# Four-direction selective scan with a mixture of experts and attention behind it: the row directions first and last, the normalisation of a batch's tokens in two halves

## The chip, the cores and the metric

The kernel runs on one core of a Trainium2 chip, in one launch. The metric is the device time of that core in microseconds; a kernel is run several times and the median counts. All data are float32.

## The reference, cut to what matters

The input is 4 images of 384 channels and 32 x 32 places; the 1024 places are the tokens. Two layers follow each other.

```python
xs = stack([x0, x1, x0[::-1], x1[::-1]])      # 4 directions: rows, columns, both reversed
dt, Bs, Cs = projections of xs per direction   # dt through softplus
h = h * exp(dt * A) + (dt * u) * B             # per token, 16 states for each channel
y = sum_n h * C
y = y0 + y2[::-1] + transpose(y1 + y3[::-1])   # the four directions added at their places
x = x + gelu(layernorm(y) * w + b)             # layer 0, first part
x = x + sum over 2 of 4 experts: gate * (gelu(ln(x) W1 + b1) W2 + b2)
x = x + attention(ln(x))                       # layer 1: 8 heads, q = k = v
x = x + kron-factored feed-forward(ln(x))
```

The sum of the directions is taken before the layer normalisation, which needs all 384 channels of a token but no other token.

## The kernel before, in words

**The scan (scan_layer, L196).** Channels lie on partitions in blocks of 32, with 4 of the 16 states beside each other. The work is a list of 32 units (L252): batch b, direction k from 0 to 3, and half i of the 1024 tokens, in which k = 0 and 1 run forward and k = 2 and 3 backward. Directions 0 and 2 go by rows and directions 1 and 3 by columns, so that a unit of 0 or 2 adds to one half of the tokens, and one of 1 or 3 to half of the columns of every row. A unit has three chunks of 128 channels (chunk, L401). In a chunk POOL multiplies dt*u by B (L432), ACT takes the exponential (L441), DVE runs the recurrence (L446), POOL or DVE multiplies by C (L460, L453), and PE adds up the states (L467) into acc; DVE adds acc into y (L294 for the first direction, L298 for the others). While a unit runs, the projection of the next one (project, L305) is made piecewise between the chunks; its results go to DRAM and come back spread over partitions (dtr, L416, and bcs, L342), on SP's queue. The PSUM of the scan is two banks "da" and a ring of two banks "ps", which acc, the projections and the normalisations take in turn.

**Between batches.** Ahead of a batch's last unit start (L223) loads and normalises the next input, in two passes of 512 tokens (layernorm, L157: mean by matmuls L164, subtraction L166, squares L173, variance L179, inverse root L150 and L151, spreading L187, multiplication L192). Behind a batch's last unit finish (L236) normalises y in two such passes, takes the GELU of 1024 tokens for each of three channel groups (L239), loads the input again (L246), adds on POOL (L247) and stores x1 to DRAM (L248). The GELU needs another table of ACT than the exponential; exp_again (L143) loads the first one again.

**The tail.** For each batch, tail_batch (L489) runs the experts, the combination, the attention and the last layers beside the scan of the next batch; for the last batch all this comes behind the scan. route (L611) calls spread (L616): it reads x1 back two token blocks at a time (L629), transposes each block on PE and takes the gate's scores (L635, L637), copies both out of the bank "p" (ACT L641, DVE L642), takes mean and variance (L643, L644), and after all eight blocks the inverse root; less_mean (L540) gives minus mean times rstd; places (L676) works out with many small DVE instructions where each token goes; and 16 indirect DMAs on POOL (L664) put the rows there. experts (L817) works through 11 slots (matmuls L889 and L905). combine (L916) fetches the results by indirect DMAs (L935) and adds them; prologue (L953) normalises, with less_mean again. attention (L974) has four steps of two heads; behind each, divide (L1026) adds the two partial sums of the softmax (L1028), inverts them and multiplies (L1045). last_layers (L1077) ends the batch.

**What sets the order.** Each engine takes its instructions in the order of its queue. The queues are made when the program is built, by a scheduler with a simulated timeline that takes ready instructions by priority; route, combine with prologue, and last_layers have a priority that is raised by 20000, and place_behind holds parts of project behind a given instruction. SBUF and PSUM tiles come from rings with a fixed number of buffers (bx 6, dtr 7, k2 6; the tail's banks s, o and p are 1 each), and the next user of a ring waits for the last one. The tail takes its tiles in the order of the program, so the routing of batch b + 1 takes its buffers behind the attention of batch b.

Of the kernel before, what the change touches and what calls it, by code (L numbers as in the profile page):

```python
# [9 lines left out]
F32 = mybir.dt.float32  # L10
I32 = mybir.dt.int32
AF = mybir.ActivationFunctionType
ALU = mybir.AluOpType
AX = mybir.AxisListType
# [3 lines left out]
P = 128  # L18
B = 4
D = 384  # L20
# [3 lines left out]
HF = 512  # L24
NH = L // HF

KG = 4
NS = 16
R = 12
XD = R + 2 * NS  # L30

NE = 4
# [16 lines left out]
MB = L // P  # L49
# [61 lines left out]
def halves(i):  # L111
    return slice(i * HF, (i + 1) * HF)


class Body:
# [80 lines left out]
    def scan_layer(self, x1, between):  # L196

        nc, tc, a = self.nc, self.tc, self.a
        with ExitStack() as ctx:
            wp = ctx.enter_context(tc.tile_pool(name="s_w", bufs=1))  # L200
            work = ctx.enter_context(tc.tile_pool(name="s_work", bufs=1))
# [31 lines left out]
                self.layernorm(x, x, self.eps6, psum, work, parts=[0])  # L233
                return x

            def finish(b, y):  # L236
                self.layernorm(y, y, self.eps5, psum, work)
                for c in range(DC):
                    ins = nc.scalar.activation(  # L239
                        y[:, c, :], y[:, c, :], AF.Gelu,  # L240
                        bias=self.col("lnb", c), scale=self.col("lnw", c),
                    ).ins
                    rows = slice(c * P, (c + 1) * P)
                    for i in range(NH):
                        x = work.tile([P, HF], F32, tag="k2", name="x", bufs=6)
                        nc.sync.dma_start(out=x, in_=a["x"][b][rows, halves(i)])  # L246
                        nc.gpsimd.tensor_add(x, x, y[:, c, halves(i)])  # L247
                        nc.sync.dma_start(out=x1[b][rows, halves(i)], in_=x)  # L248
                self.exp_again(ins)


            units = [  # L252
                (b, k, i)
                for b in range(B)
                for k in range(KG)
                for i in (range(NH) if k < 2 else reversed(range(NH)))
            ]
            us = {0: start(0)}
# [7 lines left out]
            for n, unit in enumerate(units):  # L266
                b, k, i = unit
                fed, ahead = ahead, []
                project = iter(())
                if n + 1 < len(units):  # L270
                    nb = units[n + 1][0]
                    if nb not in us:
                        us[nb] = start(nb)
                    project = self.project(units[n + 1], us[nb], wx, work, dram, psum, ahead)
                    next(project)
                if n % NH == 0:
                    carry = wp.tile([P, NB * NG], F32, tag=f"carry{n // NH % 2}", name="carry")
                if k == 0 and i == 0:
                    y = work.tile([P, DC, L], F32, tag="y", name="y")
                for c in range(DC):  # L280
                    acc = psum.tile([P, HF], F32, tag="ps", name="acc")
                    for _ in self.chunk(
                        unit, n % NH == 0, c, fed, carry, nega, sel, acc, work, dap
                    ):
                        next(project, None)
                    if k % 2 == 0:
                        ys = y[:, c, halves(i)]
                        out = acc
                    else:
                        w = slice(i * (HW // NH), (i + 1) * (HW // NH))  # L290
                        ys = y[:, c, :].rearrange("p (h w) -> p h w", h=HW)[:, :, w]
                        out = acc.rearrange("p (w h) -> p h w", h=HW)
                    if k == 0:
                        nc.vector.scalar_tensor_tensor(  # L294
                            ys, us[b][:, c, halves(i)], dsum[:, c : c + 1], out, op0=ALU.mult, op1=ALU.add
                        )
                    else:
                        nc.vector.tensor_add(ys, ys, out)  # L298
                if k == KG - 1 and b not in self.under_way:
                    self.under_way[b] = fed[2]  # L300
                if n + 1 == len(units) or units[n + 1][0] != b:
                    finish(b, y)
                    between(b)

    def project(self, unit, u, wx, work, dram, psum, made):  # L305

# [233 lines left out]
    def less_mean(self, mean, rstd, room, tag):  # L540

        less = room.tile([P, MB], tag, "less")
        self.nc.vector.scalar_tensor_tensor(less, mean, -1.0, rstd, op0=ALU.mult, op1=ALU.mult)
        return less


# [69 lines left out]
    def spread(self, b, x1, room):  # L616


        nc = self.nc
# [4 lines left out]
        sc = room.tile([P, MB, NE], "sc", "sc")  # L624


        for m in range(0, MB, 2):
            x = room.tile([P, DC, 2 * P], "k4", "x")
            nc.sync.dma_start(out=x, in_=src[:, :, m * P : (m + 2) * P])  # L629
            xt = room.tile([P, 2, D], "k4", "xt")  # L630
            for o in range(2):
                ps = room.bank("p", "tt_ps")
                cols = slice(o * P, (o + 1) * P)
                for c in range(DC):
                    nc.tensor.transpose(ps[:, c * P : (c + 1) * P], x[:, c, cols], self.ident)  # L635
                for c in range(DC):
                    nc.tensor.matmul(  # L637
                        ps[:, D : D + NE], x[:, c, cols], self.wg[:, c, :],
                        start=(c == 0), stop=(c == DC - 1),
                    )  # L640
                nc.scalar.copy(xt[:, o, :], ps[:, :D])  # L641
                nc.vector.tensor_copy(sc[:, m + o, :], ps[:, D : D + NE])  # L642
                nc.vector.bn_stats(st[:, m + o, :], xt[:, o, :])  # L643
                nc.vector.bn_aggr(mv[:, m + o, :], st[:, m + o, :])  # L644
            nc.sync.dma_start(out=self.tokens(b)[:, m : m + 2, :], in_=xt)
# [328 lines left out]
    def attention(self, xc, sums, room):  # L974
# [50 lines left out]

        def divide(t, att):  # L1026
            inv = room.tile([P, 2 * MB], "inv", "inv")
            nc.vector.tensor_add(inv, sums[:, t, :, 0], sums[:, t, :, 1])  # L1028
            nc.vector.reciprocal(inv, inv)
            ps = room.bank("p", "inv_ps")  # L1030
            nc.tensor.matmul(ps[: 2 * MB, :P], inv, self.ident, start=True, stop=True)
            rows = room.tile([2 * MB, P], "inv_rows", "inv_rows")
            nc.vector.tensor_copy(rows, ps[: 2 * MB, :P])
            for i in range(NH):
                ps = room.bank("p", "bc_ps")
                for j in range(HF // P):
                    m = i * (HF // P) + j
                    for o in range(2):
                        at = 2 * m + o
                        nc.tensor.matmul(  # L1040
                            ps[o * HD : (o + 1) * HD, j * P : (j + 1) * P],
                            self.ident[: 2 * MB, at : at + 1].to_broadcast([2 * MB, HD]),
                            rows, start=True, stop=True,
                        )
                nc.vector.tensor_mul(att[:, halves(i)], att[:, halves(i)], ps)  # L1045
# [370 lines left out]
```

## Time and profile before

| | us |
|---|---|
| median of 3 runs | 4451.01 |
| lowest and highest | 4446.85, 4462.27 |
| the profiled execution's own time | 4452.07 |
| its span, first to last instruction | 4450.2 |

| engine | busy us | share of the span |
|---|---|---|
| PE (matmul) | 3462.1 | 78% |
| POOL | 3050.0 | 69% |
| DVE | 2980.1 | 67% |
| ACT | 2469.7 | 55% |

| place in the span | us |
|---|---|
| last add into y, batch 0, 1, 2, 3 | 759, 1678, 2644, 3569 |
| first expert matmul, batch 0, 1, 2, 3 | 935, 1995, 3046, 3696 |
| first score of the attention (L1015), batch 0, 1, 2, 3 | 1462, 2520, 3567, 4195 |

Read the second table with the third: the shares are means over a first part in which the scan runs (to 3570 us) and a last one in which it has ended. A typical unit beside no tail takes 83 to 91 us (batch 0), beside the experts 97 to 108, and the longest are those at a change of batch (161 and 163 us for the first units of batches 1 and 2).

### The profile page before, as it was taken

What the parts mean: (1) busy time and instruction counts of PE and PEld (TensorE: products, weight loads), DVE (VectorE), ACT (ScalarE), POOL (GpSimd) and SP (SyncE); (2) the same over time, 40 slices, a digit from 0 to 9 for tenths busy, and PEclk for the clock granted to TensorE, in tenths of its full rate; (3) what the DMA queues carried; (4) which work ended last, traced back from release to release, by engine and by line L of the source; (5) the groups of instructions that cost most, each with busy time, mean ns of one, the idle gap of its engine ahead of it and who ended that gap; (6) DMA issues with size and microseconds to landing.
All of it is one profiled execution on the core that took longest, in us unless ns stands there. A gap on an engine that the chain in (4) does not pass through costs nothing. (4 is left out here: it accounts for less than half of the span.)

```text
span 4450.2 us, 47090 instructions
## 1 busy us (share of the span) xinstructions
PE 3462.1 (78%) x13980; PEld 1644.5 (37%) x13980; DVE 2980.1 (67%) x4252; ACT 2469.7 (55%) x4380; POOL 3050.0 (69%) x1475
## 2 busy tenths in 40 slices
PE   6545554579995887669998688758998699999897
PEld 2111111245552222325555222214555334566333
DVE  5889998778887876978787777988787720020002
ACT  4545554456664766466666477466666453325354
POOL 4999999689988877779888689879888710000100
PEclk7766665579997998679999899869999899999898
DMA  4444453468785533357779434446778534344300
GB/s 121 119 124 114 129 162 91 134 225 233 217 253 169 164 93 116 117 174 217 209 229 274 134 99 120 123 145 193 215 212 261 171 106 139 123 135 164 102 17 15
DMA packets 404760, 684.81 MB, mean 154 GB/s; under 512 B 50960, under 2 KB 206480, under 8 KB 404496
## 3 DMA queue, kind: packets, MB, share of 16 engines
q1 hardware_dynamic: 395184, 655.37, 50.0%
q0 software_dynamic: 8192, 25.17, 1.7%
q8 instruction: 112, 1.84, 0.2%
q14 instruction: 152, 1.25, 0.1%
q10 hardware_dynamic: 1120, 1.18, 0.1%
HBM read 561.47 MB, written 120.06 MB: 153 GB/s over the span
## 5 line engine op out<-in xcount | busy, mean ns | idle before, releaser
L432 POOL TENSOR_TENSOR bx<-dtr,bcs 128x1024 f32<-128x1024 f32 x768 | 1793.5, 2362 | 211.5 <-PE acc L467 118.2
L441 ACT ACTIVATE da<-dtr,nega 128x512 f32<-128x512 f32 x1536 | 1045.8, 691 | 1013.9 <-DVE bx L453 637.7
L460 POOL TENSOR_TENSOR bx<-bx,bcs 128x1024 f32<-128x1024 f32 x384 | 904.0, 2360 | 216.9 <-DVE bx L446 94.9
L467 PE MATMUL acc<-bx,sel 128*32 128x512 f32 x3072 | 518.6, 712 | 304.2 <-POOL bx L460 258.4
L889 PE MATMUL h_ps<-xc,w 128*128 128x256 f32 (+1 forms) x3168 | 665.2, 364 | 43.6 <-DVE xc L871 21.1
L905 PE MATMUL y_ps<-w,hs 128*128 128x384 f32 x1824 | 644.1, 505 | 44.3 <-ACT hs L898 40.3
L889 PEld LDWEIGHTS h_ps<-xc,w 128*128 128x128 f32 x3168 | 547.4, 196 | 228.6 <-issue 92.0
L446 DVE TENSOR_TENSOR_SCAN bx<-da,carry,bx 128x512 f32<-128x512 f32 x384 | 473.9, 1269 | 125.1 <-ACT da L441 61.9
L446 DVE TENSOR_TENSOR_SCAN da<-da,carry,bx 128x512 f32<-128x512 f32 x384 | 477.3, 1273 | 70.6 <-ACT da L441 61.3
L446 DVE TENSOR_TENSOR_SCAN bx<-da,bx 128x512 f32<-128x512 f32 x384 | 451.8, 1209 | 102.6 <-POOL bx L432 61.3
L453 DVE TENSOR_TENSOR bx<-da,bcs 128x512 f32<-128x512 f32 x768 | 511.3, 680 | 4.5
L446 DVE TENSOR_TENSOR_SCAN da<-da,bx 128x512 f32<-128x512 f32 x384 | 455.7, 1219 | 74.5 <-ACT da L441 62.9
L905 PEld LDWEIGHTS y_ps<-w,hs 128*128 128x128 f32 x1824 | 348.6, 196 | 339.6 <-issue 78.2
L1020 ACT ACTIVATE ex<-s_ps 128x512 f32<-128x512 f32 x512 | 299.2, 590 | 207.1 <-PE s_ps L1015 206.1
L1015 PE MATMUL s_ps<-w 64*128 64x512 f32 x1024 | 307.6, 675 | 83.0 <-ACT ex L1020 83.0
L467 PEld LDWEIGHTS acc<-bx,sel 128*32 128x32 f32 x3072 | 78.6, 116 | 606.1 <-POOL bx L460 371.0
L1064 PE MATMUL o_acc<-ex,vt 128*64 128x512 f32 x1024 | 295.3, 657 | 0.6 <-ACT att L1072 0.5
L894 ACT ACTIVATE hs<-h_ps,bb 128x256 f32<-128x256 f32 (+1 forms) x528 | 193.6, 449 | 148.5 <-PE h_ps L889 148.3
L1105 POOL TENSOR_TENSOR xt<-xt,wb 128x3072 f32<-128x3072 f32 x4 | 26.7, 6686 | 310.4 <-DMA wb<-in_wb 310.4
L909 DVE TENSOR_TENSOR y<-y_ps,bb 128x384 f32<-128x384 f32 x76 | 41.6, 548 | 244.0 <-PE y_ps L905 244.0
L926 POOL TENSOR_TENSOR diag<-ident,g_picked 128x1024 f32<-128x1024 f32 x8 | 15.0, 1895 | 243.1 <-PE xc_ps L868 223.8
L1015 PEld LDWEIGHTS s_ps<-w 64*128 64x128 f32 x1024 | 80.9, 192 | 257.6 <-ACT ex L1020 153.4
(215 smaller groups left out, 4026.3 us busy)
## 6 DMA issues: line engine op xcount, KB each, us to landing
w<-in_w SPq DMA_DIRECT2D x352, 576.0 KB
dtr<-dd SPq DMA_DIRECT2D x1536, 128.0 KB
bcs<-rows SPq DMA_DIRECT2D x512, 128.0 KB
dd<-one_e SPq DMA_DIRECT2D x96, 256.0 KB
dd<-mag SPq DMA_DIRECT2D x96, 256.0 KB
rows<-zero SPq DMA_DIRECT2D x76, 192.0 KB
xs<-rows SPq DMA_DIRECT2D x32, 384.0 KB
made<-y SPq DMA_DIRECT2D x32, 384.0 KB
```

Source lines behind the costliest of these rows:

```text
L432: pool = nc.gpsimd.tensor_mul(bx, dtr[q][1], bc[:, 0].unsqueeze(1).to_broadcast([P, 2, HF])).ins
L441: nc.scalar.activation(da, dtr[q][0][:, j, :], AF.Exp, scale=nega[:, col : col + 1])
L446: nc.vector.tensor_tensor_scan(run(h), run(da), run(bx[:, j, :]), 0.0 if first else hold, ALU.mult, ALU.add,)
L453: dve = nc.vector.tensor_mul(bx[:, j, :], h, cg).ins
L460: pool = nc.gpsimd.tensor_mul(bx, bx, cg.unsqueeze(1).to_broadcast([P, 2, HF])).ins
L467: nc.tensor.matmul(acc[lo : lo + DB, :], sel, out[q][:, j, :], start=(g == 0), stop=(g == NG - 1),)
L889: nc.tensor.matmul(ps[:, r, :], w1[(f + r) // wf][:, c, (f + r) % wf * P : ((f + r) % wf + 1) * P], xc[:, c, :], start=(c == 0), stop=(c = ...
L894: nc.scalar.activation(hs[:, f + r, :], ps[:, r, :], AF.Identity, bias=bb[:, f + r : f + r + 1])
L905: nc.tensor.matmul(out[:, :D], hs[:, f, t * P : (t + 1) * P], w2[f // wf][:, f % wf, :], start=(f == 0), stop=(f == FC - 1),)
L1015: nc.tensor.matmul(ps[:, o, :], w[rows, j * P : (j + 1) * P], w[rows, halves(i)], start=True, stop=True,)
L1020: ins = nc.scalar.activation(ex[:, o, :], ps[:, o, :], AF.Exp, scale=HD**-0.5, accum_out=sums[:, t, 2 * j + o, i : i + 1],).ins
L1064: ins = nc.tensor.matmul(out[cols, :], made[t][1][:, j, cols], ex[:, o, :], start=(j == 0), stop=(j == MB - 1),).ins
```

## The change

Four things are changed.

1. The directions are taken in the order 0, 1, 3, 2 (ORDER), so that the last one goes by rows, backwards: its first unit completes tokens 512 to 1023, its second one tokens 0 to 511.
2. finish takes a half i and is called after each of the two units of the last direction: one normalising pass, three GELUs on 512 columns, three loads, adds and stores, and a table load back. Its first call stands ahead of the batch's last unit.
3. spread reads the token blocks 4 to 7 before 0 to 3. In batch 0 a pair of blocks goes into the double bank "s" and is copied out by one ACT and one DVE instruction.
4. less_mean copies rstd to PSUM by ACT before its DVE instruction, and divide adds the two sums by a reduction instead of an addition of two operands.

The working out of the places is as it was.

```diff
 KG = 4
+ORDER = (0, 1, 3, 2)
...
-            def finish(b, y):
-                self.layernorm(y, y, self.eps5, psum, work)
+            def finish(b, y, i):
+                self.layernorm(y, y, self.eps5, psum, work, parts=[i])
                 for c in range(DC):
                     ins = nc.scalar.activation(
-                        y[:, c, :], y[:, c, :], AF.Gelu,
+                        y[:, c, halves(i)], y[:, c, halves(i)], AF.Gelu,
                         bias=self.col("lnb", c), scale=self.col("lnw", c),
                     ).ins
                     rows = slice(c * P, (c + 1) * P)
-                    for i in range(NH):
-                        x = work.tile([P, HF], F32, tag="k2", name="x", bufs=6)
-                        nc.sync.dma_start(out=x, in_=a["x"][b][rows, halves(i)])
-                        nc.gpsimd.tensor_add(x, x, y[:, c, halves(i)])
-                        nc.sync.dma_start(out=x1[b][rows, halves(i)], in_=x)
+                    x = work.tile([P, HF], F32, tag="k2", name="x", bufs=6)
+                    nc.sync.dma_start(out=x, in_=a["x"][b][rows, halves(i)])
+                    nc.gpsimd.tensor_add(x, x, y[:, c, halves(i)])
+                    nc.sync.dma_start(out=x1[b][rows, halves(i)], in_=x)
                 self.exp_again(ins)
...
-                for k in range(KG)
+                for k in ORDER
...
-                if k == KG - 1 and b not in self.under_way:
-                    self.under_way[b] = fed[2]
-                if n + 1 == len(units) or units[n + 1][0] != b:
-                    finish(b, y)
-                    between(b)
+                if k == ORDER[-1]:
+                    self.under_way.setdefault(b, fed[2])
+                    finish(b, y, i)
+                    if n + 1 == len(units) or units[n + 1][0] != b:
+                        between(b)
...
         less = room.tile([P, MB], tag, "less")
-        self.nc.vector.scalar_tensor_tensor(less, mean, -1.0, rstd, op0=ALU.mult, op1=ALU.mult)
+        ps = room.bank("p", "less_ps")[:, :MB]
+        self.nc.scalar.copy(ps, rstd)
+        self.nc.vector.scalar_tensor_tensor(less, mean, -1.0, ps, op0=ALU.mult, op1=ALU.mult)
...
-        for m in range(0, MB, 2):
+        for m in [*range(MB // 2, MB, 2), *range(0, MB // 2, 2)]:
...
+            both = room.two("tt_ps") if b == 0 else None
             for o in range(2):
-                ps = room.bank("p", "tt_ps")
+                ps = room.bank("p", "tt_ps") if both is None else both[:, o, :]
...
-                nc.scalar.copy(xt[:, o, :], ps[:, :D])
-                nc.vector.tensor_copy(sc[:, m + o, :], ps[:, D : D + NE])
+                if both is None:
+                    nc.scalar.copy(xt[:, o, :], ps[:, :D])
+                    nc.vector.tensor_copy(sc[:, m + o, :], ps[:, D : D + NE])
+            if both is not None:
+                nc.scalar.copy(xt, both[:, :, :D])
+                nc.vector.tensor_copy(sc[:, m : m + 2, :], both[:, :, D : D + NE])
+            for o in range(2):
...
-            nc.vector.tensor_add(inv, sums[:, t, :, 0], sums[:, t, :, 1])
+            nc.vector.tensor_reduce(inv, sums[:, t], AX.X, ALU.add)
```

## The prediction

> **What bounds the kernel now.** I read the page's forty slices first, then busy time by stretch, the list of waits, and the timelines of the places that the diff touches.
>
> ```profile
> PE   6545554579995887669998688758998699999897
> DVE  5889998778887876978787777988787720020002
> POOL 4999999689988877779888689879888710000100
> PEclk7766665579997998679999899869999899999898
> ```
>
> A slice is 111 us. Up to slice 32 (3570 us) POOL and DVE are busy: the scan. From there PE is at 9. So two chains run side by side: the scan (32 units, paced by POOL and DVE) and the tail (experts, attention, last layers of the batch before). The program ends when PE has done what tail work is left when the scan ends.
>
> ```profile
> 3575.00:3600.00 25.00, 25.00 (x115) 13.85 (x114) 3.77 (x6) 10.14 (x26) 0.00 (x0) 0.94 0.22 72
> ...
> 3675.00:3700.00 25.00, 17.30 (x64) 7.08 (x63) 1.39 (x3) 7.03 (x24) 5.48 (x6) 0.86 0.61 236
> 3700.00:3725.00 25.00, 25.00 (x121) 14.48 (x119) 1.66 (x3) 8.83 (x24) 0.00 (x0) 1.00 0.26 72
> ```
>
> Columns: stretch, its length, then busy us of PE, weight loads, DVE, ACT, POOL. Behind the scan PE is full but for some 17 us between 3600 and 3700, in which the last batch is normalised and routed. So what counts is (a) when the scan ends, (b) how far the tail has come by then, (c) those 17 us.
>
> The last output add of batch 0 is at 759.1 us; then, by the timeline:
>
> ```profile
> 759.88 4.76 PE L164 MATMUL ln_mean<-y,ones 128*128 128x512 f32 x6 [0.89 <-DVE y L298]
> ...
> 778.75 1.87 DVE L192 TENSOR_TENSOR y<-y,ln_rows 128x512 f32<-128x512 f32 x3
> ...
> 793.97 7.41 POOL L247 TENSOR_TENSOR x<-x,y 128x512 f32<-128x512 f32 x6 [16.22 <-ACT y L239]
> ...
> 809.46 0.90 PE L635 MATMUL tt_ps<-ident,x 128*128 128x128 f32 x3 [9.12 <-DMA x<-x]
> ```
> ```profile
> 935.14 5.49 PE L889 MATMUL h_ps<-xc,w 128*128 128x256 f32 x12 [1.05 <-DVE xc L871]
> ```
>
> Two normalising passes, one per half of the tokens, come one behind the other (760 to 781, then to 794), then the GELU, the adds, the write of x1, its re-reading, eight transposing rounds to 842, the places, the indirect writes, and 176 us after the last add the first expert matmul. The tail is a serial chain from there: experts 935 to 1383, attention to 1775, routing of the next batch, experts 1995, 3046. So a lead won at 935 is carried to 3570.
>
> ```profile
> 1426.00 12.68 DVE L543 SCALAR_TENSOR_TENSOR less<-mv,rstd 128x8 f32<-128x8 f32 x1 [0.61 <-ACT rstd L151]
> ```
> ```profile
> 1425.90 4.63 POOL L432 TENSOR_TENSOR bx<-dtr,bcs 128x1024 f32<-128x1024 f32 x2
> 1430.51 1.25 POOL L388 TENSOR_TENSOR lnw<-lnw,mag 128x512 f32<-128x512 f32 x1
> 1431.73 6.92 POOL L432 TENSOR_TENSOR bx<-dtr,bcs 128x1024 f32<-128x1024 f32 x3
> 1441.19 2.35 POOL L460 TENSOR_TENSOR bx<-bx,bcs 128x1024 f32<-128x1024 f32 x1 [2.54 <-DVE bx L446]
> ```
>
> An instruction on 8 numbers a partition holds DVE for 12.68 us: exactly until POOL, after three multiplies without a gap, pauses at 1438.6. Then POOL in its turn waits for the scans.
>
> ```profile
> 2817.36 10.53 DVE L1028 TENSOR_TENSOR inv<-sums 128x16 f32<-128x16 f32 x1 [0.98 <-ACT ex L1020]
> ```
> ```profile
> 1599.89 7.01 POOL L432 TENSOR_TENSOR bx<-dtr,bcs 128x1024 f32<-128x1024 f32 x3 [24.05 <-PE acc L467]
> ```
>
> The first is the same in the attention's division. The second is the scan's own loss: ahead of a batch's last unit the next input gets two normalising passes, and the accumulator of that unit comes behind them in a ring of two PSUM banks.
>
> **What the Trainium skill says.** SBUF — State Buffer, section "Who interferes with whom": a DVE instruction with two SBUF inputs is blocked whole by a GpSimd instruction that reads SBUF; one with at most one SBUF input isn't, and tensor_reduce never is. The trace agrees: L543 (two SBUF inputs) 12.68 us against 0.15 at its best, while L453 (one input in PSUM) has a mean of 680 ns beside a busy POOL. ScalarE: Activation LUTs, section "What ACT_TABLE_LOAD costs": a load of about 1283 ns, 2.66 us for a switch with its drain; here the load is 1283 ns, a drain is not shown.
>
> **The change, part by part.** *Smaller stalls in DVE.* In less_mean one input moves to PSUM, in divide two become one reduce. L543 took 12.68, 11.62 and 10.80 us in the scan's time, 0.15 otherwise: 34.6 us gone, less three ACT copies of 128x8 (0.2 us each, from L151) and a hand-over (below 0.4 us): 33 us of the tail's chain. The copy waits for the single bank "p", which nothing else holds there. L1028: 10.53 once, 1.84, 1.42, 2.35 and 0.49 in other divisions; only each attention's last is on the tail's chain: 10 us. For the scan these stalls are worth POOL's idle time behind them: 12.5 us after 1438, 5.4 at 2510, 8.5 at 2836, 12.2 after 3547, together 38.6; some would have come otherwise, I take **30**.
>
> *Finish by halves.* Per half: 3 mean matmuls, 3 subtracts, 3 squares, 12 small matmuls, 2 ACT steps, 4 spreading matmuls, 3 multiplies, 3 GELUs, 3 loads and 3 stores on SP, 3 adds on POOL. Nothing but the tables is added: 4 more switches each way, 8 x 1.28 = 10 us of ACT (21 with the skill's drain, 0 where GELU neighbours GELU), hidden: ACT is 55% busy; uncovered I charge 2. Three GELUs on 512 columns instead of 1024 cost half plus overhead, +2 us in all. Behind batch 0's last add only one pass is left: the adds end at about 786 and not 801 (15 us); of the eight rounds (33 us) four are done during the last unit: 17 us. So the experts begin **32 us** earlier. A pair of rounds for one (only batch 0) saves a handover or two, counted at nothing. The re-reading of the first half needs only its own stores; if it waited for all, the 17 are lost.
>
> *Where the moved half goes.* It stands ahead of the last unit, in front of the two passes of the next input: three passes there, one after. A pass is some 14 to 16 us; 6 bx buffers cover the accumulator for about 14 (six multiplies of 2.36). Loss in sum: before 24.1 and 20.5 (input) plus 16.2, 22.5, 19.5 (finish, POOL's wait for the GELU); after, about 16 more at the first place and 16 less at the second: **0**, from -16 to +16 for each of three batches. In the last batch one pass comes into the scan unaccompanied, covered by the buffers: +4 (0 to 16). On SP the three stores wait for POOL with the dtr loads of the next chunk queued behind; cover is one chunk, about 30 us; if it is gone, 5 to 7 us each (waits seen at L432 for dtr: 5.6, 6.7).
>
> *Order of directions.* The same eight units with the same instructions: 0. The sums of units 4 to 7 swap strided for plain views (L298: 659 to 692 ns for both).
>
> **Sum**, against the profiled 4452.1 us (span 4450.2, 1.9 around it; median of the runs 4451.0). Scan's end: -30 +4 +5 (more tail beside it) = -21, at 3549. Tail: -32 -33 -10 = -75, attention of batch 2 at 3492 instead of 3567. It then has 57 us beside the scan and not 3; in 296 us of the attention before it PE did about 175 us of its matmuls (a quarter of 307.6+295.3+96.6), 0.6 per us: 54 x 0.6 = 32 us of PE work done ahead. Idle behind the scan: of 17 us I take back 6. -21 -32 -6 = -59: 4393, as median **4392**.
>
> **Rivals.** *A, the boundary stalls fall too:* the three waits of POOL for GELU (58 us) go, and the three passes overlap. For: pass 2 began at 777.8 under pass 1. Against: the ring. Another -45: 4347. *B, the lead isn't cashed:* the re-reading waits for both halves and the experts' stage, with PE at 9, eats the rest; only DVE's release counts: -25: 4426. *C, nothing to measure:* B, and the queues made anew lose 20 us: 4447. *D, slower:* the ring decides. Three passes hold the accumulator 16 us longer in three batches (+48) and 16 in the last, POOL's in-order wait for the GELU stays where it was, so nothing is given back: scan -30 +48 +16 +5 = +39. The scan's delay then reaches the routing of batch 1, which has only some 60 us between x1 (1727) and its first transpose (1792): the tail is gated and loses its lead but for some 25 us x 0.6 = 15. +24: 4475. It decides when POOL's waits ahead of the last units pass about 40 us in each batch with the later ones at 20 as before.
>
> **Chances.** Forecast 0.45 (own range 4358 to 4415), A 0.15, B 0.15, C 0.10, D 0.15. About 0.3% (13 us) is what a measurement can tell here. Faster 0.75, same 0.10, slower 0.15. The range goes from A's middle, 4340, to just short of D, 4460.
>
> **What would show it.** L543 and L1028 at 0.2 us everywhere; first L889 near 903; adds of batch 0's second half done by 790; attention of batch 2 near 3490; last scan near 3550. Wrong if POOL's wait ahead of the last unit grows past 40 us while the one behind it stays, or if the first half's transposes come no earlier than the second's.

## The result and the profile after

| | before | after |
|---|---|---|
| median, us | 4451.24 (13 runs) | 4440.3 (13 runs) |
| lowest and highest | 4446.85, 4466.64 | 4429.68, 4447.66 |
| the profiled execution, its span | 4452.07, 4450.2 | 4435.07, 4433.2 |
| ratio to before, 95% interval | | 0.9966 [0.9957, 0.9975] |

The change gains 11 us in the medians and 17 between the two profiled executions. The forecast was 59: right in sign, wrong in size. The forty slices of the kernel after, in the same order of rows as before:

```profile
PE   6545555479886887579987888569998789999797
DVE  5889997878777868968786857977878740020002
POOL 4999996889878968788888859678988931000100
PEclk7766665589997998689998888769999899999898
```

The picture is the same: a scan up to slice 32, then a full PE. Taking the same marks in both traces (last add into y, first expert matmul, first score matmul) shows where the parts of the sum went:

| us in the span | before | forecast | after |
|---|---|---|---|
| last add of batch 0 | 760 | 760 | 793 |
| first expert matmul, batch 0 | 935 | 903 | 922 |
| first score, batch 0 / 1 / 2 | 1462 / 2520 / 3567 | – / – / 3492 | 1441 / 2468 / 3522 |
| last add of batch 3 (the scan's end) | 3570 | 3549 | 3582 |
| last matmul of the last experts | 4146 | 4087 | 4129 |

Busy time by stretch, from the scan's end to the last expert matmul (columns: stretch, its length, then busy us of PE, weight loads, DVE, ACT, POOL, the granted clock, DMA share, GB/s), first of before:

```profile
3570.00:4146.00 576.00, 555.57 (x2425) 320.88 (x2421) 72.23 (x192) 252.97 (x507) 33.33 (x25) 0.98 0.41 136
```

and of after:

```profile
3582.00:4129.00 547.00, 520.90 (x2257) 308.14 (x2255) 68.16 (x187) 230.43 (x444) 29.65 (x22) 0.97 0.42 139
```

168 matmuls fewer are left when the scan ends, and the stretch is 29 us shorter. But it begins 12 us later: -29 + 12 = -17.

**The stalls of DVE are gone.** The instructions of the two lines that took 12.68 and 10.53 us (count, then min, median and max in ns):

```profile
L547 DVE SCALAR_TENSOR_TENSOR less<-mv,less_ps x8: 147/158/164, 841.5 to 4160.0; 128x8 f32<-128x8 f32 x8
```
```profile
L1039 DVE TENSOR_REDUCE inv<-sums x16: 161/186/188, 1505.8 to 4336.5; 128x16 f32<-128x32 f32 x16
```

None is above 0.19 us, as the Trainium skill has it (SBUF — State Buffer, "Who interferes with whom": one SBUF input, or a reduction, doesn't contend).

**The changes of batch cost more.** POOL's timeline of after, at the three places ahead of a batch's last unit:

```profile
683.26 3.73 POOL L248 TENSOR_TENSOR x<-x,y 128x512 f32<-128x512 f32 x3 [3.99 <-ACT y L241]
...
715.39 13.89 POOL L434 TENSOR_TENSOR bx<-dtr,bcs 128x1024 f32<-128x1024 f32 x6 [28.41 <-PE acc L469]
...
1630.91 9.30 POOL L434 TENSOR_TENSOR bx<-dtr,bcs 128x1024 f32<-128x1024 f32 x4 [31.02 <-PE acc L469]
...
2590.37 11.62 POOL L434 TENSOR_TENSOR bx<-dtr,bcs 128x1024 f32<-128x1024 f32 x5 [41.56 <-PE acc L469]
```

The bracket is POOL's idle time ahead of the instruction and what ended it. Before, the accumulator cost 0, 24.1 and 20.5 us here and the GELU 16.2, 22.5 and 19.5 behind the unit, 103 in all; now the accumulator costs 28.4, 31.0 and 41.6 and the GELU 21 at the three places together, 122 in all. (With the small waits for the two it is 123 before and 127 after.)

**Why batch 0's last unit takes 130 us and not 91** is seen on PE. Before, the next input's two passes run beside unit 6, whose last add is at 669:

```profile
642.49 3.72 PE L164 MATMUL ln_mean<-u,ones 128*128 128x512 f32 x6 [0.43 <-DMA u<-in_x]
...
661.54 2.81 PE L164 MATMUL ln_mean<-u,ones 128*128 128x512 f32 x6 [0.20 <-PE acc L467]
```

In after, the moved pass of y stands first in the program. It needs the last add (662), and the two passes of u come behind it in the ring:

```profile
643.47 2.62 PE L165 MATMUL ln_mean<-y,ones 128*128 128x512 f32 x4
...
662.89 2.07 PE L165 MATMUL ln_mean<-y,ones 128*128 128x512 f32 x2 [0.89 <-DVE y L300]
...
678.38 4.71 PE L165 MATMUL ln_mean<-u,ones 128*128 128x512 f32 x6
...
697.63 3.62 PE L165 MATMUL ln_mean<-u,ones 128*128 128x512 f32 x6
...
710.09 4.22 PE L332 MATMUL xd_ps<-u,wx 128*44 128x512 f32 x6
714.25 2.78 PE L469 MATMUL acc<-bx,sel 128*32 128x512 f32 x24
```

The first pass of u starts 36 us later than before. From the last add of unit 6 to the accumulator three passes, 662 to 714, are in a row, and POOL, whose six bx buffers are full, waits.

### The profile page after: what moved, and what is told of

Read it like the earlier page. It is cut to its first block, busy times and chain, and to the rows that moved or that the text cites. A ratio compares the mean times of both kernels' runs of the same rounds, so it can differ in the third digit from the quotient of the medians.

```text
span 4433.2 us, 47118 instructions
## 1 busy us (share of the span) xinstructions
PE 3475.1 (78%) x13980; PEld 1661.1 (37%) x13980; DVE 2938.2 (66%) x4248; ACT 2483.9 (56%) x4404; POOL 3050.0 (69%) x1475
## 3 DMA queue, kind: packets, MB, share of 16 engines
q14 instruction: 152, 1.25, 0.1%
```

## The experiments

Runs that are compared share a chip with runs of the kernel before, which took 4451 to 4477 us from chip to chip, so that ratios compare best. A distance in us between two ratios is their difference times 4451.

| label | edit (on before or after) | median us | ratio to before, 95% |
|---|---|---|---|
| small_only | before, part 4 alone | 4450.78 | 0.999 [0.998, 1.0] |
| halves_only | after without part 4 | 4479.68 | 1.0063 [1.0044, 1.0082] |
| order_only | before, part 1 alone | 4464.55 | 1.0026 [1.0016, 1.0035] |
| both_behind | after, nothing moved into the scan | 4427.31 | 0.9945 [0.9926, 0.9965] |
| behind_start | after, moved pass behind the input's passes | 4403.17 | 0.9884 [0.9866, 0.9901] |
| own_bank | after, batch 0's moved pass in another bank | 4401.02 | 0.9877 [0.9861, 0.9893] |
| behind_chunk | after, moved pass behind a chunk of the last unit | 4450.56 | 0.9993 [0.9979, 1.0007] |
| chunk_no_small | the same without part 4 | 4521.94 | 1.0163 [1.0141, 1.0185] |
| no_first_pass | after, moved normalisation left out | 4414.21 | 0.9916 [0.9893, 0.994] |
| early_b0_b3 | behind_start in batches 0 and 3 only | 4467.32 | 1.0031 [1.0017, 1.0045] |
| early_b3 | behind_start in batch 3 only | 4429.5 | 0.995 [0.9932, 0.9968] |

**The parts by themselves.** small_only is part 4:

```diff
-        self.nc.vector.scalar_tensor_tensor(less, mean, -1.0, rstd, op0=ALU.mult, op1=ALU.mult)
+        ps = room.bank("p", "less_ps")[:, :MB]
+        self.nc.scalar.copy(ps, rstd)
+        self.nc.vector.scalar_tensor_tensor(less, mean, -1.0, ps, op0=ALU.mult, op1=ALU.mult)
...
-            nc.vector.tensor_add(inv, sums[:, t, :, 0], sums[:, t, :, 1])
+            nc.vector.tensor_reduce(inv, sums[:, t], AX.X, ALU.add)
```

> The kernel before with part 4 of the change alone (rstd through PSUM in less_mean, the reduction in divide). Theory R (the ring eats the gain: the pass of the first half stands ahead of the two passes of the next input): the stalls of part 4 are worth what was forecast, scan about -30, tail some 13 further ahead, times 0.6: about -40, 4411 (4400 to 4425). Rival T (these stalls were free time): 4440 to 4455. Rival S (any edit makes the queues anew and that decides): anywhere within 20 of 4451, with POOL's idle time in the scan no lower than the 569 us of before.

By the time alone rival T (free time) has it. But in its trace (the profiled run took 4442.69 us, 8 below its median) the scan ends at 3533 and the attention of batch 2 starts at 3535: -37 and -32, against -30 and -43 in the prediction's sum. Little of it reaches the end, because now both chains are earlier by the same and nothing more of the tail lies beside the scan; and the stretch behind the scan grew from 576 to 601 us:

```profile
3533.00:4134.00 601.00, 568.58 (x2383) 323.62 (x2385) 71.32 (x191) 251.00 (x508) 33.28 (x25) 0.96 0.40 130
```

From PE's list of waits in this stretch (us in total, times, longest):

```profile
PE y_ps L907 <- ACT hs L900: 14.8, 7, 3.0
```

where before had

```profile
PE y_ps L905 <- ACT hs L898: 2.7, 2, 2.2
```

So 12 us more of waiting for the experts' GELU, though no instruction of this stretch was changed, and 13 us more of PE busy time at a clock of 0.96 instead of 0.98. halves_only is the change without those lines.

> The changed kernel without part 4 (less_mean and divide as before). R: the ring's loss is bare, 4440 + 40 = about 4475 (4460 to 4490), POOL waiting for acc some 160 us in all as in the changed kernel. T: 4440 as the changed kernel. S: no order between the two.

It is slower than before, as theory R expected: the scan ends at 3626, 56 us later, and the attention of batch 2 starts at 3566, where it did. DVE's stall is still there (12.77 us at 1412). In the scan the two parts almost add up: -37 + 56 = +19, and the change as a whole has +12. order_only is part 1 alone (ORDER = (0, 1, 3, 2), finish as before).

> The kernel before with the directions taken in the order 0, 1, 3, 2 and nothing else; both halves still finished behind the last unit. R and T: the order is worth nothing, 4451 within 6. S: 10 to 20 off in either direction, because the queues are made anew.

+12 us where 0 was forecast, the scan's end at 3580 instead of 3570. The stretch behind it is as before (577 us). Which queue loses the 10 us was not found; as shown below, so much can come from the layout of the queues alone.

**Where the moved half stands.** In both_behind it is moved nowhere: both halves are finished behind the last unit, still one by one and the later tokens first.

```diff
-                    finish(b, y, i)
                     if n + 1 == len(units) or units[n + 1][0] != b:
+                        finish(b, y, 1)
+                        finish(b, y, 0)
                         between(b)
```

> The changed kernel with both halves finished behind the last unit, one after the other: nothing of finish is moved into the scan, all else is as changed. R: the waits are as in the kernel before (acc 24 and 21, GELU 16, 22, 20), the experts begin near 930 and not 922; the tail's lead of part 4 alone: 4445 (4432 to 4458), near the kernel with part 4 alone. If the change's gain came from the earlier first half: above the changed kernel's 4440; if the early first half costs more than it brings: below 4440.

It is 9 us below the changed kernel (the two intervals overlap; with the swap described below it is 32, and they don't). It was expected above it, at 4445, with the waits of before; the accumulator's at the second and third change of batch are 31 and 44 us, no shorter than in the changed kernel. Its first expert matmul comes at 904, as forecast for the change (903), without any half being early:

```profile
798.07 0.55 PE L642 MATMUL tt_ps<-ident,x 128*128 128x128 f32 x3
...
820.66 1.28 PE L644 MATMUL tt_ps<-wg,x 128*128 128x4 f32 x6
...
903.66 6.57 PE L901 MATMUL h_ps<-xc,w 128*128 128x256 f32 x25
```

Before, the transposes ran from 809.5 to 840. Here the first half's x1 has been added up at 787, so they begin at 798 while the second half is still under way, and the eight rounds, in pairs, need 24 us instead of 31. behind_start puts the first half between the passes of the next input and the last unit:

```diff
+                if k == ORDER[-1] and n % NH == 1:
+                    finish(b, y, 1)
                 if n % NH == 0:
...
-                    finish(b, y, i)
                     if n + 1 == len(units) or units[n + 1][0] != b:
+                        finish(b, y, i)
                         between(b)
```

> The changed kernel with one call moved: the first half is finished behind the start of the next input in the program's order, ahead of the chunks of the last unit. R: the input's two passes can again be made beside the unit before, so POOL's wait for acc falls from 163 to about 120 us and unit 7 of batch 0 from 130 to about 105 us; 4415 (4405 to 4428). If it is not the order but the number of passes ahead of acc: as the changed kernel, 4440 within 6. S: within 15 of 4440, with no relation to the wait for acc.

37 us below the changed kernel. POOL's timeline ahead of the three last units:

```profile
696.54 1.29 POOL L248 TENSOR_TENSOR x<-x,y 128x512 f32<-128x512 f32 x1 [12.66 <-ACT y L241]
...
1615.21 4.68 POOL L436 TENSOR_TENSOR bx<-dtr,bcs 128x1024 f32<-128x1024 f32 x2 [46.37 <-PE acc L471]
...
2565.76 1.28 POOL L248 TENSOR_TENSOR x<-x,y 128x512 f32<-128x512 f32 x1 [59.66 <-ACT y L241]
```

In batch 0 the wait is 12.7 instead of 28.4 + 4.0, and the unit takes 110 us instead of 130. In batches 1 and 2 the three passes are serial as ever, and the waits (46, 60) are longer than the changed kernel's (38 and 46, accumulator and GELU). own_bank leaves the order and gives batch 0's moved pass another PSUM bank, that of the tail, which is idle there.

```diff
+def ring(psum, name):
+    if isinstance(psum, Room):
+        return psum.bank("o", name)
+    return psum.tile([P, HF], F32, tag="ps", name=name)
...
-                self.layernorm(y, y, self.eps5, psum, work, parts=[i])
+                self.layernorm(
+                    y, y, self.eps5, self.room if b == 0 and i == 1 else psum, work, parts=[i]
+                )
```

> The changed kernel with one thing changed: in batch 0 the pass of the first half takes its PSUM tiles from the tail's bank o, which nothing uses at that time, and not from the scan's ring of two. Nothing else of it moves in the program. Theory R (the pass's place in the ring is what costs): POOL's 28 us of waiting for acc at 715 us go, unit 7 of batch 0 takes about 95 us and not 130, the experts begin near 900 and not 922; time 4440 - 15 to 35 = about 4415 (4405 to 4428). Rival (PE, ACT and DVE are held up by the pass itself, or POOL by the GELU): unit 7 above 115 us and 4440 within 8.

It is 39 us below the changed kernel. On PE the first pass of u runs beside unit 6 again:

```profile
643.67 3.49 PE L171 MATMUL ln_mean<-u,ones 128*128 128x512 f32 x6
...
663.09 2.07 PE L171 MATMUL ln_mean<-y,ones 128*128 128x512 f32 x2 [0.89 <-DVE y L308]
...
685.27 3.09 PE L171 MATMUL ln_mean<-u,ones 128*128 128x512 f32 x6
...
699.96 4.28 PE L340 MATMUL xd_ps<-u,wx 128*44 128x512 f32 x6
```

The unit takes 121 us, POOL's wait is 18.2 and not 28.4, the experts start at 906. Only 9 us of the 39 lie in this unit. So neither expectation fits: the unit stayed far above theory R's 95 us, on the rival's side of 115, while the time came out below R's range. A second u pass still comes behind the y pass: DVE multiplies y by its rows at 683.8 and u at 685.6, and takes the work of all three passes in one queue.

**Two more places, and the pass itself.** behind_chunk puts the first half behind the first chunk of the last unit; chunk_no_small is that without part 4.

```diff
+                    if k == ORDER[-1] and n % NH == 1 and c == 0:
+                        finish(b, y, 1)
```

> The changed kernel with the first half finished behind the first of the three chunks of the last unit, not ahead of it: two passes ahead of the first chunk's accumulator, one ahead of the second's. R (what costs is how many passes stand in one row ahead of an accumulator; six bx tiles cover one pass): POOL's waits for acc and for the GELU around the last units, 118 us in the changed kernel and 128 with the first half behind the start, fall to about 75; about 30 below the kernel with the first half behind the start: 4375 (4362 to 4390). Rival (only the hoisting of the input's passes in batch 0 mattered): 4403 within 6.

A miss: no gain over before. POOL's waits at the three changes of batch are 127 us in sum, no less than in the changed kernel (122): taken apart from the input's passes, the moved one costs a wait of its own (30.1 + 12.7 ahead of and in batch 1's last unit, 33.8 + 13.1 in batch 2). Together with part 4 taken back:

> The kernel with the first half behind the first chunk, without part 4 (less_mean and divide as before). With the ring's loss gone part 4's worth shows bare: R and the forecast of 40 for part 4: 40 above its sister, 4415. From the changed kernel and the one without part 4 (4479 against 4440) the same 40. From the kernel with part 4 alone (4 below before): 4380, as its sister.

By the ratios part 4 is worth 76 us here, 43 on top of the halves in the change (40 was expected in both), 0 to 9 on the kernel before: its worth depends on what else is late. no_first_pass leaves out the normalisation of the moved half (its GELU, loads, adds and stores stay), so its output is another.

```diff
-                self.layernorm(y, y, self.eps5, psum, work, parts=[i])
+                if i == 0:
+                    self.layernorm(y, y, self.eps5, psum, work, parts=[i])
```

> The changed kernel without the normalising pass of the first half: tokens 512 to 1023 of y go into the GELU as they are (that part of the computation is left out; the GELU, the adds and the stores stay). R: the waits ahead of the last unit fall from 32, 38 and 46 us to what two passes cost, 3, 24 and 21; scan's end about 45 to 60 earlier, time 4400 (4385 to 4412). Rival (the re-made queues or the GELU's adds are what costs): above 4425.

The scan ends at 3515, 67 us before the changed kernel's, batch 0's last unit takes 94 us, and ahead of batch 1's last unit POOL waits as it did with two passes:

```profile
680.21 1.29 POOL L249 TENSOR_TENSOR x<-x,y 128x512 f32<-128x512 f32 x1
...
1599.64 13.93 POOL L435 TENSOR_TENSOR bx<-dtr,bcs 128x1024 f32<-128x1024 f32 x6 [26.01 <-PE acc L470]
```

But only 22 us (26 in the medians) come through to the end, just short of theory R's range: the attention of batch 2 starts at 3510, so that nearly nothing of it lies beside the scan any more. Two versions ask in which batch an early half matters.

> The first half is finished early, behind the start of the next input, in the batches 0 and 3 only; in 1 and 2 both halves come behind the last unit. In 1 and 2 the routing waits for the attention and not for x1, so the early half brings nothing there. Theory G (gated): as the kernel with all first halves behind the start, 4403 within 10, since its three-pass waits in batches 1 and 2 (51 and 65 us against 50 and 61) were no longer than without. R in its strict form (every third pass costs 16): 30 us below, 4375. Rival S (the queues made anew decide): no relation.

Both were wrong. Up to the first attention it runs as behind_start does (1414 and 1411). Then the first half of batch 1 is added at 1711 and not at 1633, the transposes begin at 1748 and not at 1736, the experts at 1967 and not at 1933, the attention of batch 2 at 3540 and not at 3499. What is more, PE waits 17.6 us once for the experts' rows behind the scan. So the early half seems to count in batch 1 (that of batch 2 was put back as well), once the tail is ahead; part of the 64 us stays unexplained.

> As the last one, but early in batch 3 only. Against the kernel with both halves behind everywhere (4427) it shows what the early half brings at the end of the scan: about 6 us of idle PE, 4421 (4414 to 4428); against the one with batches 0 and 3 what it brings at the first change of batch: nothing if the experts begin near 904 in both.

Equal to both_behind within their intervals: in the last batch an early half brings nothing that is seen. Put beside early_b3, early_b0_b3 has only the early half of batch 0 more, and is 36 us slower. So that half doesn't pay by itself; with the halves of batches 1 and 2 early as well (behind_start) it is part of the gain. Why is not shown.

**Parts or layout?** A swap of two independent ACT instructions in batch 0 changes no work, but makes all queues anew.

```diff
-            nc.scalar.activation(mag, ps, AF.Abs, bias=bias)
-            nc.scalar.activation(relu, ps, AF.Relu, bias=bias)
+            if b == 0:
+                nc.scalar.activation(relu, ps, AF.Relu, bias=bias)
+                nc.scalar.activation(mag, ps, AF.Abs, bias=bias)
+            else:
+                nc.scalar.activation(mag, ps, AF.Abs, bias=bias)
+                nc.scalar.activation(relu, ps, AF.Relu, bias=bias)
```

On the kernel before:

> The kernel before with two independent ACT instructions of batch 0's projection in the other order (the part below zero and the magnitude of the same bank, same inputs, same results). No work is added, removed or moved to another unit. Theory S: the queues that the scheduler makes differ all the same, and the time by 10 to 30 us in either direction; if so, differences of that size between versions can't be put down to their parts. If not S: 4452 within 5.

It ends at 1.0014 [1.0002, 1.0026], 6 us up, though batch 0 ends 18 us earlier (742). Then on four versions, to see whether their order is one of parts or of chance:

> Batch 0's two activations of one projection step, which don't depend on each other, change places; no work changes. If the differences between the versions come from their parts, the changed kernel stays at 4440, within 8, and its last unit of batch 0 still takes about 130 us (121 or more) against 91 before. If they come from the queues being made anew at each edit, it moves by 15 us or more, in either direction, as far as the versions stood from each other.

> The same harmless swap on top of the version whose first moved pass has a bank of its own. Parts: 4401 within 8, and below the changed kernel with the swap by 30 or more. Queues made anew: moves by 15 or more, and the distance of 39 to the changed kernel shrinks to below 20 or turns round.

> The same harmless swap on top of the version in which the moved pass stands behind the next input's passes. Parts: 4403 within 8, and below the changed kernel with the swap by 29 or more. Queues made anew: moves by 15 or more, and the distance of 37 shrinks to below 20 or turns round.

> The same harmless swap on top of the version that moves nothing into the scan (both halves finished behind the last unit, half by half). Parts: 4427 within 8, some 13 below the changed kernel with the swap, and some 25 above the two versions that move the pass well. Queues made anew: the order of these three isn't kept.

| version | ratio without | ratio with the swap | moved by, us |
|---|---|---|---|
| before | 1 | 1.0014 [1.0002, 1.0026] | +6 |
| changed kernel | 0.9966 [0.9957, 0.9975] | 0.9991 [0.9977, 1.0004] | +11 |
| both_behind | 0.9945 [0.9926, 0.9965] | 0.9919 [0.9888, 0.995] | -12 |
| behind_start | 0.9884 [0.9866, 0.9901] | 0.9893 [0.9869, 0.9917] | +4 |
| own_bank | 0.9877 [0.9861, 0.9893] | 0.9874 [0.9844, 0.9904] | -1 |

In these swaps layout is worth up to 12 us either way. own_bank and behind_start stayed within the 8 us that the theory of parts allowed; the changed kernel and both_behind moved by 11 and 12, between the two theories. Batch 0's last unit takes 130 us in the changed kernel with the swap as without, 121 in own_bank both times, 112 and 110 in behind_start. The order of the four is the same in both columns: own_bank stays 39 and 52 us below the changed kernel, behind_start 37 and 44, both_behind 9 and 32. Against before without the swap the swapped changed kernel can't be told from no change; against before with it, it is 10 us below. That own_bank's gain is seen in its unit by 9 us only left one more question: it also takes three tiles fewer from the ring of two, so everyone behind it gets the other bank. One extra tile turns the ring back:

```diff
+                if b == 0 and i == 1:
+                    turn = psum.tile([P, HF], F32, tag="ps", name="turn")
+                    nc.tensor.matmul(turn[:, :P], self.ident, self.ident, start=True, stop=True)
```

> One tile more is taken from the ring of two banks ahead of batch 0's moved pass and filled by one small matmul that nobody reads, so that every later user of the ring gets the other bank of the two, with the same work else. If the version with a bank of its own gained by turning the ring (it takes three tiles fewer), this one gains as well: about 4405 on the first chip's scale, ratio to before near 0.989. If it gained by letting the next input's pass run ahead, this one stays where the changed kernel is, ratio 0.997 to 0.999.

> The same extra tile on top of the version with a bank of its own, which turns the ring back to where it is in the changed kernel. If the turn was the gain, it is lost: ratio to before near 0.997. If the freed pass was the gain, the ratio stays near 0.988.

after_turn has 0.999 [0.9982, 0.9997]: no gain, so the turn alone isn't it. own_bank_turn has 0.9925 [0.9909, 0.9942], between the two forecasts: 29 us below after_turn, but 21 above own_bank. Its units are as long as own_bank's to within a few us and its scan ends at 3560; most of the loss comes behind, in one wait of PE in the attention that own_bank doesn't have:

```profile
PE bc_ps L1061 <- DVE att L1066: 13.9, 1, 13.9
```

So the bank of its own is worth 29 to 52 us in three pairs, and how much of it arrives depends on the layout: the tile that does nothing moved own_bank by 21 us, more than any swap did.

**Where in the scan the time lies.** Here a change of batch is the last two units of a batch and the first one of the next, from last add to last add. The last column sums POOL's waits for the accumulator and the GELU at the three changes, small ones included.

| us | 0 to 1 | 1 to 2 | 2 to 3 | other units | scan's end | waits |
|---|---|---|---|---|---|---|
| before | 343 | 377 | 382 | 2468 | 3570 | 123 |
| small_only | 341 | 368 | 373 | 2451 | 3533 | 126 |
| changed kernel | 366 | 374 | 387 | 2455 | 3582 | 127 |
| no_first_pass | 341 | 355 | 366 | 2452 | 3515 | 75 |
| own_bank | 352 | 380 | 383 | 2434 | 3550 | 134 |
| behind_start | 347 | 391 | 421 | 2393 | 3552 | 138 |
| both_behind | 350 | 375 | 394 | 2435 | 3554 | 137 |

The moved pass costs 24, 19 and 21 us at the three changes (changed kernel less no_first_pass) and 3 elsewhere. At the first change own_bank and behind_start win back 13 and 18 us, with the swap 11 and 23, and own_bank with the turn 10: this much is shown. At the other two changes together they are no shorter than the changed kernel (763 and 812 against 761), and their POOL waits are no fewer. What they gain besides, 21 and 63 us, lies in units where none of these edits stands; with the swap own_bank gains 50 us at those two changes and 16 in the other units, so that not even the place is fixed. By what way it gets there is not settled.

## Why the prediction was wrong

**The model of the end held roughly.** The prediction let the end follow from the scan's end S and the start A of batch 2's attention: 0.6 us of PE work done ahead per us between them. With before's numbers that gives 0.4 S + 0.6 A + 577.5 for the last expert matmul: for after 0.4 x 3582 + 0.6 x 3522 + 577.5 = 4123.5, measured 4129; behind_start 4098 and 4100.5, own_bank 4093 and 4095. These are among the closest; the other runs end up to 29 us later than it says (small_only 22, early_b0_b3 28), with longer waits behind the scan in both. The miss of 42 us (4087 to 4129) is therefore 0.4 x 33 = 13 for the scan's end, 0.6 x 30 = 18 for the tail and 11 for the rest: PE's idle time behind the scan was to fall by 6 us, and rose by 6 (20 to 26).

**The step that failed is "Where the moved half goes: 0".** The prediction set +16 us ahead of a batch's last unit against -16 behind it. By the parts, the scan with part 4 alone ends at 3533 and with everything at 3582, so the halves and the order cost 49 us where the sum had 4 + 5: 25, 6 and 14 at the three changes of batch and 5 elsewhere. (The order by itself has 10, in order_only, of which next to nothing lies at the changes of batch.) By no_first_pass the pass cost 19 to 24 us at a change of batch and not 16; by the difference of these figures, what came back behind it was some 13 and 7 us in batches 1 and 2, and nothing in batch 0. POOL's waits say the same: those for the GELU went from 58 us to 21, as forecast, and together with the accumulator's they came out no higher in batches 1 and 2 (100 before, 91 after), but went from 24 to 36 in batch 0. There the prediction read no wait at all ahead of the unit and took +16; it became 28.

It counted the pass as one more in a row of three. It did not see that in batch 0 the input's two passes were no part of a row: they ran beside unit 6, and putting a pass that needs unit 6's last add ahead of them in a ring of two banks ties both to that add. behind_start and own_bank, which untie the input's passes in two different ways, end the scan at 3552 and 3550, where 3549 was forecast, and come to 4403 and 4401, near the forecast of 4392. But only 18 and 13 us of their gain are seen at the place that they mend, so that this agreement is in part luck.

**"The experts begin 32 us earlier"**: 13. The chain from the last add to the first expert matmul did shrink, from 175 to 129 us (46, more than the 32 forecast), but the last add came 33 us later. The forecast had held it still. These are the lines behind that add in the changed kernel:

```profile
820.91 0.90 PE L641 MATMUL tt_ps<-ident,x 128*128 128x128 f32 x3 [6.51 <-DMA x<-x]
...
828.56 0.88 PE L641 MATMUL tt_ps<-ident,x 128*128 128x128 f32 x3 [3.87 <-DMA x<-x]
```

Only two pairs of rounds are left there, as meant. The first half's four were done between 692 and 703. Yet both_behind is at 904 with all eight rounds behind the unit: of the 32 us, most is to be had by handling the halves apart and the rounds in pairs, which "counted at nothing", and little by moving a half.

**"Smaller stalls in DVE"**: the mechanism is right, the sizes nearly so. POOL's idle time that a scan of DVE or its carry ended fell from 193 to 153 us (-40; forecast -30), and small_only's scan by 37. Its tail gained 32 of 43. In small_only, though, that idle time fell to 185 only, and the rest of the 37 us came from other waits of POOL; against halves_only, which has 183, it is the forecast's 30. In the changed kernel 34 us came back as other waits of POOL, for ACT's one_e (43 to 60) and for small DVE instructions, most of them the routing's (31 to 48); the sum had this as "some would have come otherwise", at 8.6.

**"So a lead won at 935 is carried to 3570"** held only roughly. With the swap, the changed kernel had its first expert matmul at 909 and not at 922, and its third attention at 3572 and not at 3522, on a chip on which before is 25 us slower in all. In the changed kernel the lead grew from 13 us at the first experts to 49 at the second (1946), and then no more (46 at the third, 45 at the third attention), although 11.62 us at 2486 and 10.53 at 2817 were gone: the second experts and attention took 522 + 300 us to before's 525 + 296. What took their place is not shown.

**The rivals.** D named the mechanism at the last units, and 28, 31 and 42 us come near its 40; but the later waits were given back, and so its +48 is not there. C has the nearest number (4447), and its "queues made anew" are worth up to 12 us in the swaps and 21 in the turn, but the lead that it leaves out was cashed (29 us in the stretch behind the scan): it was won too small. For the same reason B (4426) is not what happened, nor is A. The change's own gain of 11 us is no larger than what the layout is worth: that its sign came out as forecast is no proof of the sum.

## What to carry to other kernels

Before putting work earlier in the program, look at what takes the same ring behind it, and ask whether that work has so far run free of the producer which the moved work must wait for; a ring hands its banks out in the order of the program, and ties the two. Here a bank of its own, or a place behind the free work, helped: own_bank at 4401 us, 0.9877 [0.9861, 0.9893], is the best version found, a little below behind_start, and keeps its ratio under the harmless swap, though not with one more tile in the ring (0.9925). When the queues are made anew by each edit, repeat a comparison with an edit that changes nothing: differences below some 20 us can't be told from the layout here.

## What the runs showed of the hardware

A DVE instruction of 0.15 us with two SBUF inputs was held not only through one GpSimd instruction but, in places, through a row of them without a gap: in halves_only L545 took 12.77 us, just while POOL ran six (6.92 us for three, 1.25 for one, 4.62 for two). The Trainium skill (SBUF — State Buffer, "Who interferes with whom") has one instruction blocked by the one that has the port; that the waiting one can miss its turn between two, several times in a row, is what these traces add. It doesn't always: in the kernel before, L1028 once ended with the first of three multiplies that POOL ran without a gap.

```profile
1535.63 1.84 DVE L1028 TENSOR_TENSOR inv<-sums 128x16 f32<-128x16 f32 x1
```
```profile
1535.07 7.01 POOL L432 TENSOR_TENSOR bx<-dtr,bcs 128x1024 f32<-128x1024 f32 x3 [3.26 <-PE acc L467]
```

What decides between the two was not found.

The granted clock in the full stretch behind the scan was 0.98 with PE idle for 20 us (before) and 0.95 with 46 (early_b0_b3), but also 0.98 with 40 (early_b3) and 0.96 with 32 (small_only): PE's idle time in the stretch alone doesn't fix it.
